# Opening of a linear attention with y and z in single pieces, attention steps of the first batch moved by one, and the last sum joined to its norm

## The chip, the cores and the metric

The kernel runs on one core of one Trainium2 chip. The metric is the device time of one execution in microseconds (us). The times shown are the median of three runs and one more execution under the hardware profiler. Five engines work side by side: TensorE (PE, with its weight loads listed as PEld), VectorE (DVE), ScalarE (ACT), GpSimd (POOL) and SyncE (SP, which issues DMAs). Each runs its own instructions in the order in which the program issues them, and waits on semaphores for the others.

## The reference

Eight batches of 512 tokens with 128 channels pass a linear attention and then a dense mixture of eight experts, each behind norms:

```python
x = x + layernorm(attn(layernorm(x)))      # attn has a norm, softmax and residual of its own
x = x + layernorm(ffn(layernorm(x)))

# attn: 4 heads of 32
xn = (x - mean) / sqrt(var + EPS) * gamma + beta
q, k, v = split(xn @ w_qkv)
q = q * 32 ** -0.5
k = softmax(k, over the tokens)
out = ((k.T @ v) applied to q) @ w_out + b_out
return out + x

# ffn: every token goes through all 8 experts, 128 -> 512 -> 128
for wg, wu, wd in experts:
    acc = acc + (silu(x @ wg) * (x @ wu)) @ wd
```

All data are float32. Inputs and weights are random; gamma, beta and b_out are not trivial.

## The kernel before, in words

**Stages.** A batch is worked on as 4 groups (NJ) of 128 tokens, tokens on the partitions in the attention, channels on the partitions in the experts. The experts are 32 steps (8 experts by 4 slices of 128 hidden units). A step multiplies the transposed tokens zT by a slice of wg (g, L902) and of wu (u, L903), 512 columns at once; ACT takes Silu of g into sg (L905); DVE multiplies by u into h (L926). The down projections are gathered over 16 steps and then run together in `down_pairs` (L797) from h and from sums `t` of pairs of h that POOL makes (L940 to L942); sums of the down weights, `ws`, are made once (`weight_sums`, L755). A bank of PSUM holds one g or u; the tags g and u have two banks each, the tag ps two, accA and accB one each. In the half steps every third step takes accA and accB in place of g and u.

**Units.** The list `units` first has batch 0 for steps 0 to 15, its first 256 tokens and then its second 256 (the half steps, 256 columns wide), then batch 0 whole for steps 16 to 31, then the batches 1 to 6 whole, and batch 7 whole up to step 24 and in halves after that.

**Opening.** `opening()` runs the attention of batch 0 directly, in an order written by hand, for both halves, as far as the first half's zT. Its parts: the norms of x (`pair_stats`), keys and their maximum (kmax, L370), exp (L373), values, context (c_ps), the matrix m (L418) that joins context and output weights, and then, for each half, the generator `after_m`, whose stages are separated by `yield`: the residual in y's bank by an identity matmul (L631), y by qT and m (L634), y's statistics (`norm_stats`, L177 to L183), the covariance of x and y, from which the next norm's scale rstd2 is had without statistics of x2 (L648 to L658), the normed yn and the sum x2 (L661), z (`norm_apply`, L252), z's transposes (L261) and the copies into zT (L671 and L673). `next(first)` and `next(second)` run one stage of a half. `keep_warm` issues matmuls whose results are not read, and `prepare` derives small weights for the later batches. The statistics of batch 1 (`bn`, `moments`, `powers`) are also computed in the opening.

**Plan.** `plan` gives, for every unit, a list of calls for each step. They are issued after the step's g, u, sg and h, and before the down projections that fall due. In the first unit they run the second half's stages, then batch 1's attention: norm, turn (32x32 transposes on DVE and a bounce through DRAM by SP), bias, affine, keys (key product, kmax, exp and the turn of the exponentials), with weight sums of the experts 0 to 4 on POOL in between. In the second unit four stages of `context` follow, and in the third `values` and the norms after it. Exp and Silu are in different activation tables, so that ACT loads a table before and after the keys' exp.

**End.** The last half of batch 7 is gathered in an `End` with one bank for each of its two groups. `finish` takes the statistics of both, norms them on DVE, adds x2 on POOL (group 0) and DVE (group 1), and stores them through the queues of SP and ACT.

Of the kernel before, what the change touches and what calls it, by code (L numbers as in the profile page):

```python
# [9 lines left out]
F32 = mybir.dt.float32  # L10
# [6 lines left out]
def kernel(  # L17
# [40 lines left out]
    nc = tc.nc  # L58
# [80 lines left out]
    def prepare():  # L139


        t = ps_acc.tile([P, N], F32, tag="accB", name="w_ps")
        nc.tensor.transpose(t[:, :C], w_qkv_sb[:, 0:C], ident)
        nc.scalar.mul(wqT, t[:, :C], QSCALE)
        nc.scalar.mul(gwv, w_qkv_sb[:, 2 * C : 3 * C], gamma_sb)
        yield
        nc.tensor.matmul(t[:, :1], w_qkv_sb[:, 2 * C : 3 * C], beta_sb, start=True, stop=True)
        bv = const.tile([P, 1], F32, name="bv")
        nc.scalar.copy(bv, t[:, :1])
        bvw = work.tile([P, C], F32, tag="gs", name="bvw")  # L150
        nc.scalar.mul(bvw, w_out_sb, bv)
        yield
        nc.tensor.matmul(t[:, :C], heads, bvw, start=True, stop=True)
        nc.scalar.copy(mb, t[:, :C])
        yield
# [57 lines left out]
    def scales(stats, name, pair=False):  # L213
        return powers(*moments(stats, name, pair), name)

    def moments(stats, name, pair=False):
        n = 2 * NJ if pair else NJ
        mv = small.tile([P, NJ, 2], F32, tag=f"mv{NJ}", name=f"mv_{name}")
        for j in range(NJ):
            nc.vector.bn_aggr(mv[:, j, :], stats[:, j, :])  # L220
        ve = small.tile([P, n], F32, tag=f"sve{n}", name=f"ve_{name}")
        nc.vector.tensor_scalar_add(ve[:, :NJ], mv[:, :, 1], EPS)
        if pair:
            nc.vector.scalar_tensor_tensor(
                ve[:, NJ:], ve[:, :NJ], EPS, mv[:, :, 1], ALU.mult, ALU.add
            )
        nm = small.tile([P, n], F32, tag=f"snm{n}", name=f"nm_{name}")
        for i in range(0, n, NJ):
            nc.vector.tensor_scalar(nm[:, i : i + NJ], mv[:, :, 0], -1.0, None, ALU.mult)  # L229
        return ve, nm  # L230

    def powers(ve, nm, name):


        n = ve.shape[1]
        rstd = small.tile([P, n], F32, tag=f"srstd{n}", name=f"rstd_{name}")
        nc.gpsimd.tensor_tensor(rstd, ve, mhalf[:, :n], ALU.pow)  # L237
        nc.gpsimd.tensor_tensor(nm, nm, rstd, ALU.mult)
        return rstd, nm
# [58 lines left out]
    def flat(t):  # L298
        return t.rearrange("p j c -> p (j c)")
# [3 lines left out]
    def opening():  # L303
# [19 lines left out]
        z = work.tile([P, NJ, C], F32, tag="z", name="z_0")  # L323
        zT = zp.tile([P, NQ, NJ, Q], F32, tag="zT", name="zT_0")
        kmax = small.tile([P, 3], F32, tag="kmax0", name="kmax_0")
# [12 lines left out]

        keep_warm(warm, 5)
        keep_warm(w_qkv_sb[:, : N // 2])  # L340
        nc.scalar.copy(junk, warm[:, :1])
# [21 lines left out]

        first_norm(0)
        for h in H:
            k_ps.append(bank(f"k_ps{h}", "ps" if h else "u"))
            nc.tensor.matmul(
                k_ps[h][:, :W], w_qkv_sb[:, C : 2 * C], xnT[:, COL[h]], start=True, stop=True
            )
            nc.vector.tensor_reduce(kmax[:, h : h + 1], k_ps[h][:, :W], AX.X, ALU.max, negate=True)  # L370
        nc.vector.tensor_tensor(kmax[:, 2:3], kmax[:, 0:1], kmax[:, 1:2], ALU.min)
        for h in H:
# [4 lines left out]
        for h in H:  # L377
# [7 lines left out]
            nc.vector.tensor_copy(v[:, COL[h]], v_ps[h][:, :W])  # L385
        next(first)
        for h in H:
            t = bank(f"ek_ps{h}", "u" if h else "g")
# [14 lines left out]
        nc.scalar.mul(qT[:, COL[0]], q_ps[0][:, :W], QSCALE)  # L403

        after = attentions[1] = Attention(1)
        after.s = bn(after.x[:, :3], "1_1")
        ctxT = work.tile([P, C], F32, tag="ctxT", name="ctxT_0")
# [8 lines left out]
        nc.vector.reciprocal(rsum, ksum[:, 2:3])  # L416
        bn(after.x[:, 3:], "1_1", after.s, 3)
        nc.vector.tensor_scalar(m, m_ps[:, :C], rsum, None, ALU.mult)  # L418
        next(first)
        next(second)  # L420
        next(second)
        moment = moments(after.s, "1_1", pair=True)
        weights = prepare()
# [7 lines left out]
        next(first)  # L431
        after.sc = powers(*moment, "1_1")
        keep_warm(flat(yn[:, J[0]]), 2)
        next(first)
        for _ in first:
# [34 lines left out]
    class Attention:  # L470
# [26 lines left out]

        def keys(self):
            b = self.b
            k_ps = ps.tile([P, N], F32, tag="ps", name=f"k_ps_{b}")  # L500
            nc.tensor.matmul(k_ps, w_qkv_sb[:, C : 2 * C], self.xnT, start=True, stop=True)  # L501
            kmax = small.tile([P, 1], F32, tag="kmax", name=f"kmax_{b}")
            nc.vector.tensor_reduce(kmax, k_ps, AX.X, ALU.max, negate=True)
            ekT = work.tile([P, N], F32, tag="ekT", name=f"ekT_{b}")
            ksum = small.tile([P, 1], F32, tag="ksum", name=f"ksum_{b}")
# [54 lines left out]
    class Last:  # L560
# [6 lines left out]
        def blocks(self):  # L567
# [3 lines left out]
                t.rearrange("p a (s j k) -> p a s j k", s=2, j=2),  # L571
                self.sums[len(self.f)].rearrange("c (s a j i) -> c a s j i", s=2, a=NQ, j=2),
            )
# [47 lines left out]
    def after_m(h, lo, hi, xt, s1, qT, m, x1b, x2, yn, z, zT):  # L621
# [4 lines left out]
        n = hi - lo  # L626
        pool, tag = (ps_gu, "u") if lo else (ps, "ps")
        y_ps = pool.tile([P, N], F32, tag=tag, name=f"y_ps_0_{lo}")
        for j in range(lo, hi):
            cols = slice((j - lo) * C, (j - lo + 1) * C)  # L630
            nc.tensor.matmul(y_ps[:, cols], ident, x1b[:, j, :], start=(j == lo), stop=False)  # L631
        yield
        for j in range(lo, hi):
            nc.tensor.matmul(  # L634
                y_ps[:, (j - lo) * C : (j - lo + 1) * C], qT[:, j * P : (j + 1) * P], m,
                start=False, stop=(j == hi - 1),
            )
        y = y_ps[:, : n * C].rearrange("p (j c) -> p j c", c=C)
        yield
# [5 lines left out]
        mv, rstd, ve = norm_stats(y, f"3_0_{lo}", keep=True)  # L645
        yield
        for j in range(n):
            nc.vector.scalar_tensor_tensor(  # L648
                z[:, lo + j], xt[:, lo + j], mvx[:, j, 0:1], y[:, j], ALU.subtract, ALU.mult,
                accum_out=cov[:, j : j + 1],  # L650
            )
        nc.vector.tensor_scalar(cov, cov, 2.0 / C, None, ALU.mult)
        nc.vector.reciprocal(rv, ve)
        nc.vector.tensor_tensor(rv, rv, mv[:, :, 1], ALU.mult)
        nc.vector.tensor_tensor(rv, rv, vex[:, :n], ALU.add)
        nc.gpsimd.tensor_tensor(t, rstd, cov, ALU.mult)
# [7 lines left out]
        yield  # L664
        norm_apply(z[:, r], x2[:, r], (mvx, rstd2))
        yield
        z_ps = transpose4(flat(z[:, r]), f"z_ps_0_{lo}")
        for j in range(1 if lo else n):
            cp = nc.vector.tensor_copy if j else nc.scalar.copy
            if lo:  # L670
                cp(zT[:, :, r], by_block(z_ps[:, : n * P], n))  # L671
            else:
                cp(zT[:, :, j], z_ps[:, j * P : (j + 1) * P].rearrange("c (a i) -> c a i", a=NQ))  # L673
        zTs[0] = zT

    class End:
# [42 lines left out]
        def finish(self):  # L719
# [4 lines left out]
            dst = out[b].rearrange("(p j) c -> p j c", j=NJ)  # L724
            s = [norm_stats([f], f"5_{b}_{self.lo + j}") for j, f in enumerate(self.f)]
            for j, f in enumerate(self.f):
                norm_apply([fn[:, j]], [f], s[j])
                (nc.vector if j else nc.gpsimd).tensor_tensor(
                    o[:, j, :], fn[:, j, :], x2s[b][:, self.lo + j], ALU.add
                )  # L730
                (nc.scalar if j else nc.sync).dma_start(dst[:, self.lo + j], o[:, j, :])
# [69 lines left out]
    def plan(b, lo, begin):  # L801
# [18 lines left out]
        if b == 0 and begin == 0:  # L820
            if not lo:
                second = rest.pop()
                go = lambda: next(second, None)
                at(0, go, a.norm)
                at(1, go)
                at(3, a.turn)
                at(4, go)
                at(6, go)
                at(8, go)
                for i, e in enumerate((0, 1, 2, 3, 4)):  # L830
                    at(2 + 2 * i, lambda e=e: weight_sums(nc.gpsimd, [e]))
                at(9, a.bias)
                at(13, a.affine)
                at(14, a.keys)
            else:
                for i in range(12, 16):
                    at(i, a.context)
# [28 lines left out]
        else:  # L866
            at(16, a.values)
            at(17, a.stats3, a.scales3, second.stats, second.scales, a.residual)
            at(17, lambda: weight_sums(nc.vector, [5, 6, 7]), second.norm, second.turn)
# [10 lines left out]
    for n, (b, lo, hi, begin, end) in enumerate(units):  # L880
        if lo == begin == 0 and b + 2 < B:
            xs[b + 2] = load_x(b + 2)
        zT = zTs[b][:, :, lo:hi]
        whole = hi - lo == NJ
        last = b == B - 1 and not whole
        cols = (hi - lo) * P
        if whole:
            zT = zT.rearrange("c a (h j) i -> c h a (j i)", h=2)
# [91 lines left out]
```

## Time and profile before

| what | us |
|---|---|
| median of 3 runs (lowest, highest) | 693.56 (693.36, 693.69) |
| the profiled execution | 693.51 |
| its span, first to last instruction | 691.60 |
| PE busy in the span | 682.9 |
| first expert matmul (L902) | 19.53 |
| last matmul ends, about | 686.6 |
| last DMA issue starts | 688.97 |

Start times in the profile count from the span's start. A line of the order of time gives start, length, engine, line and operation with output and inputs, the count of instructions that were merged, and in brackets how long the engine had been idle and who released it. Matmuls of float32 show as two instructions for one matmul of the program. Busy time of engines that nobody waits for does not set the time.

### The profile page before, as it was taken

The page shows a single profiled execution, that of the slowest core. Times are in us where ns is not written, and L with a number is a line of the kernel's source. Part 1 is how long each engine was busy: PE and PEld are TensorE (multiplying, and loading weights), DVE is VectorE, ACT ScalarE, POOL GpSimd, SP SyncE. Part 2 cuts the span into 40 slices and gives each one's busy share as a digit, 9 for nine tenths or more (in the row PEclk, how much of TensorE's full clock was granted, in tenths as well). Part 3 has the DMA queues.
Part 4 walks back from the last instruction along what each step waited for, and adds up shares of the span by engine and source line. Part 5 has one row for each costly group of instructions (what it writes and reads, how often), then busy time and mean ns, then how long its engine had stood idle before and what let it go on. Part 6 is the DMA issues. An engine that isn't in the chain of part 4 may idle for free.

```text
span 691.6 us, 9214 instructions
## 1 busy us (share of the span) xinstructions
PE 682.9 (99%) x3175; PEld 374.3 (54%) x3175; DVE 298.3 (43%) x810; ACT 247.9 (36%) x475; POOL 424.6 (61%) x524
## 2 busy tenths in 40 slices
PE   9999999999999999999999999999999999999997
PEld 6786455454554545545455544545445454544576
DVE  6656433543236432563325624256332534134135
ACT  4552441433424333344332434244351423122221
POOL 4779773767548574495726766377673857546521
PEclk9999999999999999999999999999999999999999
DMA  8610201020010200102001010111001010010010
GB/s 265 196 31 1 76 20 58 16 93 0 31 61 1 92 0 31 61 16 78 0 31 61 30 65 0 51 41 57 22 16 63 14 47 1 1 61 1 15 55 24
DMA packets 36672, 30.82 MB, mean 45 GB/s; under 512 B 3985, under 2 KB 28049, under 8 KB 36625
## 3 DMA queue, kind: packets, MB, share of 16 engines
q1 hardware_dynamic: 36336, 30.03, 13.5%
q8 instruction: 25, 0.41, 0.2%
q10 hardware_dynamic: 288, 0.20, 0.1%
q14 instruction: 23, 0.18, 0.1%
HBM read 18.42 MB, written 11.80 MB: 44 GB/s over the span
## 4 chain that ended last, share of the span: by engine, by line
PE 96%; DVE 1%; ACT 1%; DMA 0%; issue 0%; POOL 0%; DVEq 0%; ACTq 0%
PE g L902 32%; PE u L903 31%; PE accA L797 16%; PE accB L797 12%; PE y_ps L528 1%; PE g_ps L443 1%; PE k_ps L501 1%; PE end L699 1%; DMA x<-in_L_attn_x_dram 0%; PE end_A L699 0%; ACT xh L245 0%; PE wa_ps L464 0%; PE end_B L699 0%; PE m_ps L458 0%; PE c_ps L452 0%
## 5 line engine op out<-in xcount | busy, mean ns | idle before, releaser
L926 DVE TENSOR_TENSOR h<-sg,u 128x512 f32<-128x512 f32 (+1 forms) x264 | 172.6, 655 | 352.0 <-PE u L903 340.4
L905 ACT ACTIVATE sg<-g 128x512 f32<-128x512 f32 (+1 forms) x280 | 156.3, 560 | 377.7 <-PE g L902 353.8
L902 PE MATMUL g<-zT,wg 128*128 128x512 f32 (+1 forms) x560 | 267.5, 559 | 1.4 <-ACT sg L905 0.7
L903 PE MATMUL u<-zT,wu 128*128 128x512 f32 (+1 forms) x560 | 265.7, 556 | 0.9 <-DVE h L926 0.9
L940 POOL TENSOR_TENSOR t<-h 128x512 f32<-128x512 f32 x124 | 157.2, 1268 | 158.4 <-DVE h L926 158.4
L903 PEld LDWEIGHTS u<-zT,wu 128*128 128x128 f32 x560 | 106.1, 190 | 115.2 <-issue 109.5
L902 PEld LDWEIGHTS g<-zT,wg 128*128 128x128 f32 x560 | 101.2, 190 | 98.9 <-issue 95.6
L797 PE MATMUL accB<-t,ws 128*64 128x256 f32 x496 | 138.2, 381 | 0.0
L797 PE MATMUL accA<-h,wd 128*64 128x256 f32 x496 | 128.1, 381 | 0.0
L941 POOL TENSOR_TENSOR t<-h,t 128x256 f32<-128x256 f32 x124 | 90.1, 726 | 9.7
L942 POOL TENSOR_TENSOR t<-h,t 128x256 f32<-128x256 f32 x124 | 90.0, 726 | 9.7
L797 PEld LDWEIGHTS accA<-h,wd 128*64 128x64 f32 x496 | 66.6, 137 | 45.2 <-issue 6.4
L797 PE MATMUL accB<-h,ws 128*64 128x256 f32 x248 | 73.8, 379 | 0.0
L797 PE MATMUL accA<-t,ws 128*64 128x256 f32 x248 | 73.8, 379 | 0.0
L797 PEld LDWEIGHTS accB<-t,ws 128*64 128x64 f32 x496 | 66.6, 137 | 0.0
L237 POOL TENSOR_TENSOR rstd<-ve,mhalf 128x4 f32<-128x4 f32 (+1 forms) x28 | 32.8, 1173 | 18.4 <-DVE nm L229 16.3
L797 PEld LDWEIGHTS accB<-h,ws 128*64 128x64 f32 x248 | 34.0, 137 | 17.9
L797 PE MATMUL accB<-t,wd 128*64 128x256 f32 x124 | 36.9, 379 | 0.0
L797 PE MATMUL accA<-t,wd 128*64 128x256 f32 x124 | 36.9, 379 | 0.0
L797 PEld LDWEIGHTS accA<-t,ws 128*64 128x64 f32 x248 | 34.0, 137 | 0.0
L797 PEld LDWEIGHTS accB<-t,wd 128*64 128x64 f32 x124 | 17.0, 137 | 9.0
L516 POOL TENSOR_TENSOR x<-x,bias_sb 128x128 f32<-128x128 f32 x28 | 11.9, 455 | 15.3 <-ACT x L245 15.3
(177 smaller groups left out, 414.3 us busy)
## 6 DMA issues: line engine op xcount, KB each, us to landing
wg<-in_L_ffn_Wg_dram SPq DMA_DIRECT2D x8, 256.0 KB, 6.0
wu<-in_L_ffn_Wu_dram SPq DMA_DIRECT2D x8, 256.0 KB, 5.9
wd<-in_L_ffn_Wd_dram SPq DMA_DIRECT2D x8, 256.0 KB, 6.1
bounce<-f_blkA SPq DMA_DIRECT2D x8, 256.0 KB, 2.0
fA<-bounce SPq DMA_DIRECT2D x32, 64.0 KB, 2.0
bounce<-f_blkB SPq DMA_DIRECT2D x8, 256.0 KB, 2.1
fB<-bounce SPq DMA_DIRECT2D x32, 64.0 KB, 2.0
x<-in_L_attn_x_dram SPq DMA_DIRECT2D x7, 256.0 KB, 2.8
```

What stands on the lines that cost most here:

```text
L237: nc.gpsimd.tensor_tensor(rstd, ve, mhalf[:, :n], ALU.pow)
L443: nc.tensor.matmul(g_ps[:, :C], xh[:, j, :], ek[:, :, j * Q : (j + 1) * Q], start=(j == 0), stop=(j == NJ - 1),)
L501: nc.tensor.matmul(k_ps, w_qkv_sb[:, C : 2 * C], self.xnT, start=True, stop=True)
L516: nc.gpsimd.tensor_tensor(self.x1[:, j], self.x1[:, j], bias_sb, ALU.add)
L797: nc.tensor.matmul(o, w, r, start=start, stop=stop)
L902: nc.tensor.matmul(g_ps[:, :cols], wg_sb[e][:, w], zT, start=True, stop=True)
L903: nc.tensor.matmul(u_ps[:, :cols], wu_sb[e][:, w], zT, start=True, stop=True)
L905: nc.scalar.activation(sg[:, :cols], g_ps[:, :cols], AF.Silu)
L926: nc.vector.tensor_tensor(flat(h), sg[:, :cols], u_ps[:, :cols], ALU.mult)
L940: nc.gpsimd.tensor_tensor(t2[:, 0:2], h2[:, 1::2], h2[:, 0:2], ALU.subtract)
L941: nc.gpsimd.tensor_tensor(t2[:, 2], h2[:, 3], t2[:, 0], ALU.subtract)
L942: nc.gpsimd.tensor_tensor(t2[:, 3], h2[:, 2], t2[:, 2], ALU.subtract)
```

## The change

In the opening, the first half's y is kept in two banks, one for each group of 128 tokens (ps and accB), and its z is normed, transposed and copied one group after the other, through a bank each; zT of batch 0 is laid out group by group, and the way in which the sums of batch 0 are read back at its end follows that. w_ps of `prepare` goes from accB to a g bank. The small operations on rv in `after_m` come ahead of the products for cov. The statistics of batch 1 are taken in four single steps between other work, and `moments` and `powers` become `scales` again, called ahead of m. One warm-up matmul on w_qkv becomes one on a constant.

In the plan, the second half's stages come at the steps 0, 2, 5, 7, 10 in place of 0, 1, 4, 6, 8, and batch 1's turn at 4 in place of 3. The key product with its maximum stays at step 14, and exp with what follows goes to step 15. The contexts come at 13, 14, 15 and 16 in place of 12 to 15, and the values at 17 in place of 16.

In `finish`, ACT computes mean minus f while POOL computes the scale, and one DVE instruction multiplies by the scale and subtracts the product from x2.

```diff
     def prepare():
-        t = ps_acc.tile([P, N], F32, tag="accB", name="w_ps")
+        t = ps_gu.tile([P, N], F32, tag="g", name="w_ps")
...
     def scales(stats, name, pair=False):
-        return powers(*moments(stats, name, pair), name)
...
-        return ve, nm
-
-    def powers(ve, nm, name):
...
     def opening():
...
-        zT = zp.tile([P, NQ, NJ, Q], F32, tag="zT", name="zT_0")
+        zT = zp.tile([P, NJ, NQ, Q], F32, tag="zT", name="zT_0")
...
-        keep_warm(warm, 5)
-        keep_warm(w_qkv_sb[:, : N // 2])
+        keep_warm(warm, 6)
...
         first_norm(0)
+        after = attentions[1] = Attention(1)
+        after.s = bn(after.x[:, :1], "1_1")
         for h in H:
...
             nc.vector.tensor_reduce(kmax[:, h : h + 1], k_ps[h][:, :W], AX.X, ALU.max, negate=True)
+            if h == 0:
+                bn(after.x[:, 1:2], "1_1", after.s, 1)
...
         next(first)
+        bn(after.x[:, 2:3], "1_1", after.s, 2)
         for h in H:
             t = bank(f"ek_ps{h}", "u" if h else "g")
...
         nc.scalar.mul(qT[:, COL[0]], q_ps[0][:, :W], QSCALE)
-
-        after = attentions[1] = Attention(1)
-        after.s = bn(after.x[:, :3], "1_1")
+        bn(after.x[:, 3:], "1_1", after.s, 3)
...
         nc.vector.reciprocal(rsum, ksum[:, 2:3])
-        bn(after.x[:, 3:], "1_1", after.s, 3)
+        after.sc = scales(after.s, "1_1", pair=True)
         nc.vector.tensor_scalar(m, m_ps[:, :C], rsum, None, ALU.mult)
         next(first)
         next(second)
         next(second)
-        moment = moments(after.s, "1_1", pair=True)
         weights = prepare()
...
         next(first)
-        after.sc = powers(*moment, "1_1")
         keep_warm(flat(yn[:, J[0]]), 2)
-        next(first)
         for _ in first:
             pass
...
     def after_m(h, lo, hi, xt, s1, qT, m, x1b, x2, yn, z, zT):
...
+        if lo:
+            y_ps = ps_gu.tile([P, N], F32, tag="u", name=f"y_ps_0_{lo}")
+            y = pieces(y_ps[:, : n * C].rearrange("p (j c) -> p j c", c=C))
+        else:
+            banks = [(ps, "ps"), (ps_acc, "accB")]
+            y = [p.tile([P, N], F32, tag=t, name=f"y_ps_{t}")[:, :C] for p, t in banks]
+        for j in range(n):
+            nc.tensor.matmul(
+                y[j], ident, x1b[:, lo + j, :], start=(lo == 0 or j == 0), stop=False
+            )
+        yield
+        for j in range(n):
+            nc.tensor.matmul(
+                y[j], qT[:, (lo + j) * P : (lo + j + 1) * P], m,
+                start=False, stop=(lo == 0 or j == n - 1),
+            )
         yield
...
-        for j in range(n):
-            nc.vector.scalar_tensor_tensor(
-                z[:, lo + j], xt[:, lo + j], mvx[:, j, 0:1], y[:, j], ALU.subtract, ALU.mult,
-                accum_out=cov[:, j : j + 1],
-            )
-        nc.vector.tensor_scalar(cov, cov, 2.0 / C, None, ALU.mult)
         nc.vector.reciprocal(rv, ve)
         nc.vector.tensor_tensor(rv, rv, mv[:, :, 1], ALU.mult)
         nc.vector.tensor_tensor(rv, rv, vex[:, :n], ALU.add)
+        for j in range(n):
+            nc.vector.scalar_tensor_tensor(
+                z[:, lo + j], xt[:, lo + j], mvx[:, j, 0:1], y[j], ALU.subtract, ALU.mult,
+                accum_out=cov[:, j : j + 1],
+            )
+        nc.vector.tensor_scalar(cov, cov, 2.0 / C, None, ALU.mult)
...
+        else:
+            for j in range(n):
+                norm_apply([z[:, j]], [x2[:, j]], (mvx[:, j : j + 1], rstd2[:, j : j + 1]))
+                t = (ps_gu if j else ps).tile([P, N], F32, tag="g" if j else "ps", name=f"z_ps_0{j}")
+                nc.tensor.transpose(t[:, :P], z[:, j], ident)
+                (nc.vector.tensor_copy if j else nc.scalar.copy)(
+                    zT[:, j], t[:, :P].rearrange("c (a i) -> c a i", a=NQ)
+                )
...
     def finish(self):
...
-            s = [norm_stats([f], f"5_{b}_{self.lo + j}") for j, f in enumerate(self.f)]
+            s = []
             for j, f in enumerate(self.f):
-                norm_apply([fn[:, j]], [f], s[j])
-                (nc.vector if j else nc.gpsimd).tensor_tensor(
-                    o[:, j, :], fn[:, j, :], x2s[b][:, self.lo + j], ALU.add
+                s.append(norm_stats([f], f"5_{b}_{self.lo + j}"))
+                nc.scalar.activation(
+                    fn[:, j], f, AF.Identity, bias=s[j][0][:, 0, 0:1], scale=-1.0
+                )
+            for j in range(self.n):
+                nc.vector.scalar_tensor_tensor(
+                    o[:, j, :], fn[:, j], s[j][1], x2s[b][:, self.lo + j], ALU.mult, ALU.subtract,
+                    reverse1=True,
                 )
                 (nc.scalar if j else nc.sync).dma_start(dst[:, self.lo + j], o[:, j, :])
...
                 at(0, go, a.norm)
-                at(1, go)
-                at(3, a.turn)
-                at(4, go)
-                at(6, go)
-                at(8, go)
+                at(2, go)
+                at(4, a.turn)
+                at(5, go)
+                at(7, go)
+                at(10, go)
...
-                at(14, a.keys)
+                at(14, a.product)
+                at(15, a.softmax)
             else:
-                for i in range(12, 16):
+                for i in range(13, 16):
                     at(i, a.context)
...
-            at(16, a.values)
-            at(17, a.stats3, a.scales3, second.stats, second.scales, a.residual)
+            at(16, a.context)
+            at(17, a.values, a.stats3, a.scales3, second.stats, second.scales, a.residual)
```

Not shown are the split of `keys` into `product` and `softmax`, the unchanged path of `after_m` for the second half, and the indexing of zT and of the sums of batch 0.

More of the change, by code (lines that the diff above doesn't have):

```diff
@@ L213, in scales @@
     def scales(stats, name, pair=False):
-        return powers(*moments(stats, name, pair), name)
-    def moments(stats, name, pair=False):
         n = 2 * NJ if pair else NJ
@@ L229, in moments @@
             nc.vector.tensor_scalar(nm[:, i : i + NJ], mv[:, :, 0], -1.0, None, ALU.mult)
-        return ve, nm
-    def powers(ve, nm, name):
-        n = ve.shape[1]
         rstd = small.tile([P, n], F32, tag=f"srstd{n}", name=f"rstd_{name}")
@@ L498, in keys, with product @@
         def keys(self):
+            self.product()
+            self.softmax()
+        def product(self):
             b = self.b
@@ L503, in keys, with softmax @@
             nc.vector.tensor_reduce(kmax, k_ps, AX.X, ALU.max, negate=True)
+            self.k = k_ps, kmax
+        def softmax(self):
+            b = self.b
+            k_ps, kmax = self.k
             ekT = work.tile([P, N], F32, tag="ekT", name=f"ekT_{b}")
@@ L571, in blocks @@
                 t.rearrange("p a (s j k) -> p a s j k", s=2, j=2),
-                self.sums[len(self.f)].rearrange("c (s a j i) -> c a s j i", s=2, a=NQ, j=2),
+                self.sums[len(self.f)].rearrange(
+                    "c (s a j i) -> c a s j i" if self.b else "c (s j a i) -> c a s j i",
+                    s=2, a=NQ, j=2,
+                ),
             )
@@ L626, in after_m @@
         n = hi - lo
[L627 to L631, printed above, removed]
+        if lo:
[8 more added lines that the diff above has]
+            )
         yield
-        for j in range(lo, hi):
+        for j in range(n):
             nc.tensor.matmul(
-                y_ps[:, (j - lo) * C : (j - lo + 1) * C], qT[:, j * P : (j + 1) * P], m,
-                start=False, stop=(j == hi - 1),
+                y[j], qT[:, (lo + j) * P : (lo + j + 1) * P], m,
+                start=False, stop=(lo == 0 or j == n - 1),
             )
-        y = y_ps[:, : n * C].rearrange("p (j c) -> p j c", c=C)
         yield
@@ L646, in after_m @@
         yield
+        nc.vector.reciprocal(rv, ve)
+        nc.vector.tensor_tensor(rv, rv, mv[:, :, 1], ALU.mult)
+        nc.vector.tensor_tensor(rv, rv, vex[:, :n], ALU.add)
         for j in range(n):
             nc.vector.scalar_tensor_tensor(
-                z[:, lo + j], xt[:, lo + j], mvx[:, j, 0:1], y[:, j], ALU.subtract, ALU.mult,
+                z[:, lo + j], xt[:, lo + j], mvx[:, j, 0:1], y[j], ALU.subtract, ALU.mult,
                 accum_out=cov[:, j : j + 1],
@@ L652, in after_m @@
         nc.vector.tensor_scalar(cov, cov, 2.0 / C, None, ALU.mult)
-        nc.vector.reciprocal(rv, ve)
-        nc.vector.tensor_tensor(rv, rv, mv[:, :, 1], ALU.mult)
-        nc.vector.tensor_tensor(rv, rv, vex[:, :n], ALU.add)
         nc.gpsimd.tensor_tensor(t, rstd, cov, ALU.mult)
@@ L664, in after_m @@
         yield
[L665 to L673, printed above, removed]
+        if lo:
+            norm_apply(z[:, r], x2[:, r], (mvx, rstd2))
+            yield
+            z_ps = transpose4(flat(z[:, r]), f"z_ps_0_{lo}")
+            nc.scalar.copy(
+                zT[:, r], z_ps[:, : n * P].rearrange("c (j a i) -> c j a i", j=n, a=NQ)
+            )
[7 more added lines that the diff above has]
+                )
         zTs[0] = zT
@@ L882 @@
             xs[b + 2] = load_x(b + 2)
-        zT = zTs[b][:, :, lo:hi]
+        zT = zTs[b][:, :, lo:hi] if b else zTs[0][:, lo:hi]
         whole = hi - lo == NJ
@@ L886 @@
         cols = (hi - lo) * P
-        if whole:
+        if whole and b:
             zT = zT.rearrange("c a (h j) i -> c h a (j i)", h=2)
```

## The prediction

> **What bounds the kernel now.** I read the page first, then busy time by stretch, then PE's waits, then the order of time on each engine around every wait. The page's first table and clock row:
>
> ```profile
> PE 682.9 (99%) x3175; PEld 374.3 (54%) x3175; DVE 298.3 (43%) x810; ACT 247.9 (36%) x475; POOL 424.6 (61%) x524
> ...
> PEclk9999999999999999999999999999999999999999
> ```
>
> TensorE is busy 682.9 of 691.6 us at full clock. By stretches, from 57 to 686 us it is busy 629.00 of 629.00: nothing there can be shortened by the change, which alters no matmul of the experts. What can move is the opening (first L902 matmul at 19.53), the few waits up to 57 us, and the tail after the last matmul (686 to 691.6). PE's waits, us in total, times, longest:
>
> ```profile
> PE u L903 <- DVE h L926: 0.9, 2, 0.7
> ...
> PE g L902 <- ACT sg L905: 0.7, 1, 0.7
> PE g L902 <- DVE zT L673: 0.7, 1, 0.7
> ```
>
> After the first L902 these are all: two u waits (0.15 at 21.24, 0.72 at 24.82) and a g wait (38.67); the last line is the end of the opening. The chain of waits through the opening's last step (start, length, what):
>
> ```profile
> 17.65 0.34 DVE z L252
> ...
> 18.12 0.36 DVE z L252
> ...
> 18.52 0.34 PE z_ps L261
> ...
> 18.89 0.28 ACT zT L673
> ...
> 19.18 0.30 DVE zT L673
> ...
> 19.53 0.48 PE g L902
> ```
>
> The reader should see a row of single steps: both transposes, then one copy, then the other.
>
> **What the Trainium skill says.** "PSUM — Partial Sum Buffer", section "PSUM bank collisions raise a hardware error": two engines may not be in one bank at once, and dependencies are set to keep them apart. The trace agrees: DVE's copy waits 0.72 for ACT's, out of the same bank. "SBUF — State Buffer", section "Who interferes with whom": VectorE and GpSimd share a port pair, exclusively, and tensor_scalar is among the operations that can take it. The trace fits: L252's second z starts 0.47 after the first, with GpSimd's 1.64 pow (17.52) beside it. "ScalarE: Activation LUTs", section "What ACT_TABLE_LOAD costs": 1.283 us and a drain of 1.38 for every switch. The trace has the 1.28 but no drain: Silu's load at 36.94 is followed by its activation at 38.23. "TensorE: Matmul & The Clock Gate", section "Why this matters for your kernels": idle gaps over about 3 us cost the clock. No gap here or below is that long, so I price no slower matmuls.
>
> **Opening, statistics of batch 1.** One bn_stats (0.27) goes ahead of kmax 0, one ahead of kmax 1, one ahead of the ek copy: VectorE waited 0.35, 0.32 and 0.43 at these places, so they fit. The first needs batch 1's x: issued at 3.53, landing 4.5 later, 8.03. It then runs 8.05 to 8.3, kmax 0 slips from 8.07 to 8.25, and kmax 1 (8.82, when its matmul is done) holds. Cost 0, with no margin.
>
> The means and scales move ahead of m (L418). VectorE's order of time:
>
> ```profile
> 12.64 0.16 DVE L416 RECIPROCAL rsum<-ksum 128x1 f32<-128x1 f32 x1
> 12.72 0.27 DVE L210 BATCH_NORM_STATS2 stats<-x 128x6 f32<-128x128 f32 x1
> 13.12 0.35 DVE L418 TENSOR_SCALAR m<-m_ps,rsum 128x128 f32<-128x128 f32 x1
> 13.39 0.37 DVE L220 BATCH_NORM_AGGREGATE mv<-stats 128x2 f32<-128x6 f32 x4
> ```
>
> Before, four aggregates and four small operations (13.39 to 14.31) lay under y's matmuls. Now they start at 12.72 and their starts span 0.77, so with 0.08 for the last issue m starts at 13.56 and ends at 13.91; y's first matmul comes at 13.96, not 13.62: +0.34. GpSimd's pow (1.64) and product (0.20) come at 13.57 and end at 15.48, just before y's own pow needs GpSimd: 0.
>
> **Opening, y in two banks.** Both pieces were read at 14.34, after 0.68 of matmuls. Now y0 is done after 0.49 (L410's pair, alone) at 14.45, y1 at 14.67, and their statistics overlap the matmuls. ve starts at 15.24 instead of 15.08: 0.18 won of the 0.34. Keeping w_ps in a g bank, and a sixth constant warm-up in place of one on w_qkv (same width), cost nothing: the transposes that follow at 6.30 are PE work behind the same number of passes.
>
> **Opening, order of the covariance.** Before, GpSimd's first product ran at 16.13 while VectorE still did reciprocal, product and sum. Now these three come first and cov last: counted with the trace's steps (0.2 for a dependent small operation, 0.27 for a product), VectorE ends 0.13 later, and GpSimd does product, sum (0.28 each to the next) and pow (0.69) only after that. Relative to ve, z starts 0.42 later: +0.42; the lower bound is 0.1, if GpSimd takes the pair faster.
>
> **Opening, z in pieces.** From z0's start to L902 was 1.88. Now z1 starts 0.26 after z0 (as two xh of L252 do, no pow beside them), ends at 0.61, is transposed in its own bank from 0.65 to 0.98, copied from 1.01 to 1.31 while ACT's copy of the other piece is done, and L902 starts at 1.36: -0.52. **Sum of the opening: 0.34 - 0.18 + 0.42 - 0.52 = +0.06**; bounds -0.35 and +0.5.
>
> **Half steps, second half of batch 0.** cov moves from step 1 to 2. The wait at 24.82 is for h of step 3, behind h1, cov and h2; the same work in another order ends at the same time: 0. The transpose (0.70) goes from step 3 to 4 and yn (0.72) from 4 to 5. y's second half holds one of the two u banks until yn is read. VectorE: h4 25.63, transpose 25.97, h5 26.61, yn 26.94 to 27.66. u of step 7, at 27.52 now, wants that bank: 27.70, **+0.18** (0, or 1.05 if u of step 6 draws it). SP's bounce moves from 25.41 to about 26.7; its loads land by some 33, when affine (33.40) wants them: 0.
>
> GpSimd is the queue to watch:
>
> ```profile
> 26.54 0.45 POOL L755 TENSOR_TENSOR ws<-wd,ws 128x128 f32<-128x128 f32 x1
> 26.95 0.72 POOL L661 TENSOR_TENSOR x<-yn,x 128x256 f32<-128x256 f32 x1
> ```
>
> x2 (L661) stood behind one expert's weight sums; now it stands behind two, 1.78 each. pow ends at 25.78, the sums at 29.31, x2 at 30.03, and z runs to about 31.06 (0.99 for two, as at 27.70). Its transposes, moved from step 8 to 10, come up at 30.70; the second would start at 30.81 and starts at 31.10: **+0.29** (0 to 0.6). h of steps 8 to 10 wait behind z, but u of step 11, at 31.64, finds h8 done at 31.4.
>
> **Exp.** The keys' product stays at step 14, the softmax goes to 15. ACT's order of time there:
>
> ```profile
> 34.49 1.28 ACT L506 ACT_TABLE_LOAD   x1
> 36.14 0.69 ACT L506 ACTIVATE ekT<-k_ps,kmax 128x512 f32<-128x512 f32 x1 [0.37 <-DVE kmax L503]
> ...
> 36.94 1.28 ACT L905 ACT_TABLE_LOAD   x1
> ```
>
> and PE's answer to it:
>
> ```profile
> 38.67 0.70 PE L902 MATMUL g<-zT,wg 128*128 128x256 f32 x2 [0.70 <-ACT sg L905]
> ```
>
> ACT was away from 34.47 to 38.22, and PE ran three steps ahead (two g banks and the spare) plus k's 0.97: g of step 18 was late by 38.67 - 37.80 = 0.87. Now sg15 runs first (to 36.22), then load 1.28, exp and read 0.80, load 1.28: sg16 ends at 39.99 and g of step 19 starts at 40.05. PE, with k's matmul already spent, is ready at 38.67: 1.38 late, **+0.51**. The 0.37 wait for kmax is saved, but the cover of k's 0.97 is lost. Bounds: -0.3, if steps run further ahead than the banks say, and +0.8.
>
> Contexts and values one step later are the same matmuls. Pair sums on GpSimd then start about 1.3 later than 39.81; the eighth ends at 62.64 now and PE's last round of that group begins near 66: covered. The other axis order of batch 0's sums is one transpose in covered time: 0.
>
> **The end.** Before: pow of B ends at 688.18, fn (0.41), o (0.29), DMA issue at 688.97:
>
> ```profile
> 688.20 0.41 DVE L252 TENSOR_SCALAR fn_last<-end_B,mv,rstd 128x128 f32<-128x128 f32 x1 [0.20 <-POOL rstd L183]
> 688.65 0.29 DVE L728 TENSOR_TENSOR o_last<-fn_last,x 128x128 f32<-128x128 f32 x1
> ```
>
> Now ACT, idle since 685.1, subtracts the mean (about 0.4, under the pow), and one scalar_tensor_tensor follows at 688.20 (0.29 to 0.34): issue at 688.53, **-0.44** (-0.5 to -0.35). ACT pays no table load: L245's Identity at 20.55 follows Silu without one.
>
> **Sum.** 0.06 + 0.18 + 0.29 + 0.51 - 0.44 = +0.60. The profiled execution took 693.51 (span 691.60 and 1.91 around it; 0.05 under the median 693.56): 694.1. A measurement can tell about 0.2% here, 1.39 us: below 692.17 is faster, above 694.95 slower.
>
> **Rivals.** (1) The moved steps are hidden and the opening gains its lower bound: 693.51 - 0.35 - 0.44 = 692.7. For: banks or order may give PE more lead than I count. Against: the 0.70 at 38.67 shows how little lead there is. 0.30. (2) Slower: batch 1's x lands late. Its bn_stats now stands ahead of kmax on VectorE, and everything of the opening comes behind it there. From 8.05 each microsecond costs one. The weights around it take 5.2 to 6.1 from issue; at 5.9 it lands at 9.43: +1.40, 695.5. Against: it took 4.5 in this run. 0.10. (3) The y bank is drawn by u of step 6: 1.05 for 0.18, and the transposes' 0.29 vanishes: 694.7. 0.07. (4) Faster: as (1), and cov's move frees the 0.72 wait at 24.82: 692.0. Against: equal work ahead of h3. 0.04. My forecast holds 0.49.
>
> **Numbers.** Faster is (4), 0.04; slower is (2) and a tail of the forecast, 0.12; the rest, 0.84, is within 0.2%. The range takes in (1), (3) and the terms' bounds, and leaves out (2) and (4): 692.6 to 694.9.
>
> **What would show it.** m starting near 13.56; L902 near 19.6; GpSimd's L661 near 29.3; a g wait near 40 of 1.2 idle instead of 0.70; 0.4 less from the last pow to the last issue. I am wrong if z starts before 18.0, if the wait on sg shrinks, or if the first bn_stats of batch 1 waits beyond 8.3.

## The result, and the profile after

The changed kernel takes 694.84 us (median of 16 runs, 694.67 to 695.2), the kernel before 693.50 beside it. The ratio is 1.0019, with a 95% interval of 1.0012 to 1.0027: slower by 1.34 us, clear of zero, and just inside the 0.2% that the prediction had called no change. The profiled execution took 694.86, its span 692.9 us.

The page of the changed kernel has the same PE busy time and the same clock as before:

```profile
PE 682.9 (99%) x3175; PEld 374.4 (54%) x3175; DVE 298.6 (43%) x809; ACT 248.8 (36%) x477; POOL 425.7 (61%) x523
...
PEclk9999999999999999999999999999999999999999
```

So all of the difference is in waits and at the two ends. PE's waits in the changed kernel (us in total, times, longest):

```profile
PE g L925 <- ACT sg L928: 1.2, 1, 1.2
PE u L926 <- DVE h L949: 0.8, 1, 0.8
...
PE y_ps_ps L645 <- ACT qT L410: 0.5, 1, 0.5
PE g L925 <- ACT zT L687: 0.4, 1, 0.4
```

The wait of g on sg grew from 0.7 to 1.2, and y's matmuls wait where they did not; only the wait at the end of the opening is shorter. (The view puts y's wait down to ACT's qT, which is done at 13.90. But y starts 0.15 after m's end in both kernels, at 13.62 after 13.47 before and at 13.99 after 13.84 now, so m fits as what it waits for.)

The opening is best counted from the first bn_stats, which starts when batch 0's x lands: 3.48 in the profile before, 3.19 in the one after, and from 3.17 to 3.62 over all profiles of this study, for reasons that the profiles don't show. From there:

| us from the first bn_stats to | before | after |
|---|---|---|
| kmax of the second half | 5.34 | 5.61 |
| m | 9.64 | 10.31 |
| ve of y (L181) | 11.60 | 12.07 |
| z of the first group | 14.17 | 15.29 |
| first expert matmul | 16.05 | 16.71 |

VectorE at the first row. Batch 1's statistics now stand ahead of kmax, and the first of them waits for x:

```profile
8.07 0.29 DVE L210 BATCH_NORM_STATS2 stats<-x 128x6 f32<-128x128 f32 x1 [0.63 <-DMA x<-in_L_attn_x_dram]
8.28 0.41 DVE L366 TENSOR_REDUCE kmax<-k_ps 128x1 f32<-128x256 f32 x1
8.60 0.28 DVE L210 BATCH_NORM_STATS2 stats<-x 128x6 f32<-128x128 f32 x1
8.80 0.41 DVE L366 TENSOR_REDUCE kmax<-k_ps 128x1 f32<-128x256 f32 x1
```

The scales of batch 1 ahead of m, again VectorE in order of time:

```profile
13.36 0.23 DVE L228 TENSOR_SCALAR nm<-mv 128x4 f32<-128x4 f32 x2
13.50 0.34 DVE L415 TENSOR_SCALAR m<-m_ps,rsum 128x128 f32<-128x128 f32 x1
```

The chain of waits through the last part of the opening (start, length, what) now runs through POOL:

```profile
16.94 0.21 POOL cov L666
...
17.22 0.21 POOL cov L667
...
17.49 0.96 POOL cov L668
...
18.48 0.35 DVE z L245
...
18.88 0.34 PE z_ps L686
...
19.24 0.28 ACT zT L687
...
19.90 0.45 PE g L925
```

From z to the first expert matmul it takes 1.42 instead of 1.88: the pieces do what they say. But z starts late, and pow (L668) is 0.96 long, not 0.69 as before. In the half steps, POOL's x2 stands behind two experts' sums, as its order of time shows:

```profile
29.37 0.46 POOL L777 TENSOR_TENSOR ws<-wd,ws 128x128 f32<-128x128 f32 x1
29.79 0.73 POOL L671 TENSOR_TENSOR x<-yn,x 128x256 f32<-128x256 f32 x1
```

ACT around the first keys' exp, and PE's wait that follows:

```profile
36.85 0.38 ACT L928 ACTIVATE sg<-g 128x256 f32<-128x256 f32 x1 [1.37 <-PE g L925]
37.26 1.28 ACT L509 ACT_TABLE_LOAD   x1
38.55 0.69 ACT L509 ACTIVATE ekT<-k_ps,kmax 128x512 f32<-128x512 f32 x1
...
39.35 1.28 ACT L928 ACT_TABLE_LOAD   x1
```

```profile
41.08 0.70 PE L925 MATMUL g<-zT,wg 128*128 128x256 f32 x2 [1.24 <-ACT sg L928]
```

The 0.37 that exp had waited for kmax is gone, and PE waits longer all the same. At the end, one instruction stands between the last pow and the last issue:

```profile
689.73 0.35 DVE L749 SCALAR_TENSOR_TENSOR o_last<-fn_last,rstd,x 128x128 f32<-128x128 f32 x1 [0.26 <-POOL rstd L183]
690.12 0.36 ACTq L753 DMA_DIRECT2D out_dram<-o_last  x1
```

From the last round of end_A matmuls to that issue it is 3.21 us, before 3.58.

My theory after reading the two traces: the change costs in four places that do not depend on each other (scales ahead of m; the order of cov, which delays POOL in the opening and again in the half steps; the moved stages of the second half; exp one step later), and gains in two (the pieces, the end). The rival was that one lateness early in the kernel shows up again further on, so that undoing a later part alone would bring nothing.

### The profile page after: what moved, and what is told of

It is laid out like the page before. It is cut to its first block, busy times and chain, and to the rows that moved or that the text cites. A ratio compares the mean times of both kernels' runs of the same rounds, so it can differ in the third digit from the quotient of the medians.

```text
span 692.9 us, 9212 instructions
## 1 busy us (share of the span) xinstructions
PE 682.9 (99%) x3175; PEld 374.4 (54%) x3175; DVE 298.6 (43%) x809; ACT 248.8 (36%) x477; POOL 425.7 (61%) x523
## 4 chain that ended last, share of the span: by engine, by line
PE 95%; DVE 1%; POOL 1%; ACT 1%; DMA 1%; issue 1%; SPq 0%; POOLq 0%; DVEq 0%
PE g L925 32%; PE u L926 31%; PE accA L819 16%; PE accB L819 12%; PE y_ps L531 1%; PE g_ps L437 1%; PE k_ps L499 1%; DMA x<-in_L_attn_x_dram 1%; PE end L715 1%; POOL ws L777 0%; PE end_A L715 0%; POOL cov L668 0%; ACT xh L238 0%; PE end_B L715 0%; PE wa_ps L458 0%
```

## The experiments

Times are medians of 9 to 21 executions; the kernel before, beside them, took 693.52, 693.46 or 693.48. Single executions of one kernel scatter by 0.3 to 0.8 us: the changed kernel's lie between 694.67 and 695.20. With exp back, with the old order of cov and with the old stages, every execution was below that; the smaller differences rest on overlapping executions.

**The end alone**, in the kernel before (`finish` as in the change, nothing else):

```diff
-                norm_apply([fn[:, j]], [f], s[j])
-                (nc.vector if j else nc.gpsimd).tensor_tensor(
-                    o[:, j, :], fn[:, j, :], x2s[b][:, self.lo + j], ALU.add
...
+                nc.scalar.activation(
+                    fn[:, j], f, AF.Identity, bias=s[j][0][:, 0, 0:1], scale=-1.0
+                )
+            for j in range(self.n):
+                nc.vector.scalar_tensor_tensor(
+                    o[:, j, :], fn[:, j], s[j][1], x2s[b][:, self.lo + j], ALU.mult, ALU.subtract,
+                    reverse1=True,
```

> The kernel before with the changed end alone. Theory (the last issue comes earlier by the removed step): the last DMA issue starts 0.37 us sooner after the last round of end matmuls, as it did in the changed kernel (3.21 against 3.58), and the time falls by 0.37, to 693.1. Rival (part of it is lost behind the issue, since the changed kernel's span went on 2.78 us after its last issue instead of 2.63): the time falls by 0.2 only, to 693.3.

Measured: 693.26, down by 0.26 (ratio 0.9997, 0.9989 to 1.0005, so not clear of zero by itself). The issue is earlier as expected, 688.75 - 685.55 = 3.20 us after end_A. The median lies between the theory's 693.1 and the rival's 693.3. What follows the last issue is 2.46 to 2.83 us in the eleven profiles with the new end and 2.60 in the two with the old one, so that the 0.2 between theory and rival can't be settled.

**Exp at step 15 alone**, in the kernel before:

```diff
-                at(14, a.keys)
+                at(14, a.product)
+                at(15, a.softmax)
```

> The kernel before with the first keys' exp at step 15 and the key product left at step 14, nothing else. Theory (PE's lead no longer contains the key product while ACT is away): the wait of g on sg grows from 0.70 to about 1.25 us of idle, and the time rises by 0.5, to 694.0. Rival (the wait only grew in the changed kernel because its opening and half steps had pushed ACT and PE apart): 693.5, the wait stays near 0.7.

Measured: 694.04, up by 0.52. PE's waits in this kernel:

```profile
PE g L912 <- ACT sg L915: 1.2, 1, 1.2
```

**Exp back at step 14**, in the changed kernel:

```diff
-                at(15, a.softmax)
+                at(14, a.softmax)
```

> The changed kernel with exp back at step 14, nothing else. Theory: the wait of g on sg goes back to about 0.7 us of idle and the time falls by 0.55, to 694.3. Rival (as for the exp alone): no change, 694.8.

Measured: 694.33, down by 0.51, with the wait back at 0.7. The two runs agree with opposite signs, one with and one without the rest of the change: the term stands alone.

**One expert's sums ahead of x2 instead of two**, in the changed kernel:

```diff
-                for i, e in enumerate((0, 1, 2, 3, 4)):
-                    at(2 + 2 * i, lambda e=e: weight_sums(nc.gpsimd, [e]))
+                for i, e in zip((2, 6, 7, 8, 10), range(5)):
+                    at(i, lambda e=e: weight_sums(nc.gpsimd, [e]))
```

> The changed kernel with the weight sums of experts 1 to 4 issued at the steps 6, 7, 8 and 10 instead of 4, 6, 8 and 10, so that x2 stands behind one expert's sums on POOL and not two. Theory (z's transposes are late because x2 is queued behind the sums): x2 starts near 28.1 instead of 29.79, z is done before step 10, and the time falls by 0.4, to 694.4. Rival (the transposes themselves cost that at their new step, whatever z does): 694.8.

Measured: 694.60, down by 0.24. POOL reaches x2 sooner although the opening of this profile ended 0.30 later:

```profile
28.45 0.72 POOL L671 TENSOR_TENSOR x<-yn,x 128x256 f32<-128x256 f32 x1
```

The direction is that of the theory, the size is smaller, and single executions overlap (694.38 to 694.97). From u of step 10 to g of step 11 it was 0.96 in the changed kernel and is 0.65 now, as it was before at the old step; I had counted the transposes' own 0.22 as a loss. What they wait for is 0.31.

**The old order of cov**, in the changed kernel:

```diff
-        nc.vector.reciprocal(rv, ve)
-        nc.vector.tensor_tensor(rv, rv, mv[:, :, 1], ALU.mult)
-        nc.vector.tensor_tensor(rv, rv, vex[:, :n], ALU.add)
         for j in range(n):
...
         nc.vector.tensor_scalar(cov, cov, 2.0 / C, None, ALU.mult)
+        nc.vector.reciprocal(rv, ve)
+        nc.vector.tensor_tensor(rv, rv, mv[:, :, 1], ALU.mult)
+        nc.vector.tensor_tensor(rv, rv, vex[:, :n], ALU.add)
```

> The changed kernel with the order of the covariance put back (cov's products first, the operations on rv after them), nothing else. Theory (POOL's three operations wait for the last of VectorE's, and pow then meets x2's addition and takes 0.95 instead of 0.70): in the opening z comes some 0.5 us sooner after y's ve, and in the half steps POOL reaches x2 about 0.4 sooner, so that most of the lateness of z's transposes goes: together -0.8, to 694.0. Rival (order without effect, z waits for x2 anyway): 694.8.

Measured: 693.78, down by 1.06: the dearest single part. (The profile shows 0.87 of it: 0.59 in the opening and 0.28 from the first expert matmul to the last round of end_A.) From ve to z it is 2.62 instead of 3.22 (before 2.57). POOL's pow in this kernel:

```profile
17.41 0.70 POOL L668 TENSOR_TENSOR cov<-cov,mhalf 128x2 f32<-128x2 f32 x1
```

and VectorE's addition, which now comes after it:

```profile
17.67 0.43 DVE L671 TENSOR_TENSOR x<-yn,x 128x256 f32<-128x256 f32 x1
```

In the half steps x2 is sooner too (29.24), and z's transposes no longer wait (30.97, 0.40 long, where they took 0.69).

**The first statistics of batch 1 behind kmax 0**, in the changed kernel:

```diff
-        after.s = bn(after.x[:, :1], "1_1")
...
             if h == 0:
-                bn(after.x[:, 1:2], "1_1", after.s, 1)
+                after.s = bn(after.x[:, :1], "1_1")
```

and the two later calls take the groups 1, and 2 with 3.

> The changed kernel with the first bn_stats of batch 1 behind kmax 0 and the others one place later, nothing else. Theory (it waited 0.63 us for batch 1's x ahead of kmax 0, and kmax 1 came 0.27 later after the first statistics than in the kernel before): the distance from the first bn_stats to m falls from 10.31 to about 10.06 and the time by 0.25, to 694.6. Rival (kmax 1 is late for another reason, PE's): no change, 694.8.

Measured: 694.74, down by 0.10, with executions from 694.45 to 694.97, so that neither no change nor the 0.25 is ruled out. In its profile the distance to m is 10.06, as expected, so kmax 1 was late for the theory's reason there. How much it is late varies with the landing of batch 1's x. Counted from the first bn_stats, the statistics ahead of kmax could start at 4.88 to 4.91 in four profiles, the changed kernel's among them, at about 4.75 in two, and at 4.46 in the run on m below; kmax 1 is late by 0.27 to 0.30, by 0.13 to 0.17, and not at all. That may be why the time shows less than 0.25; it is not shown.

**The scales behind m**, in the changed kernel (`aggr` is the four bn_aggr, `moments` the small operations, `powers` POOL's part):

```diff
         bn(after.x[:, 3:], "1_1", after.s, 3)
+        after_mv = aggr(after.s, "1_1")
         ctxT = work.tile([P, C], F32, tag="ctxT", name="ctxT_0")
...
-        after.sc = scales(after.s, "1_1", pair=True)
         nc.vector.tensor_scalar(m, m_ps[:, :C], rsum, None, ALU.mult)
+        moment = moments(after_mv, "1_1", pair=True)
+        after.sc = powers(*moment, "1_1", part=slice(NJ, 2 * NJ))
+        after.sc_rest = lambda: powers(*moment, "1_1", part=slice(0, NJ), rstd=after.sc[0])
...
-                at(0, go, a.norm)
+                at(0, go, a.norm, a.sc_rest)
```

> The changed kernel with batch 1's bn_aggr ahead of ctxT, the rest of its scales behind m, half of the powers at once and half after the first step; nothing else. Theory (the scales ahead of m hold m back by 0.42): the distance from m_ps to m closes, the distance from the first bn_stats to the first expert matmul falls from 16.71 to about 16.3, and the time by 0.4, to 694.4. Rival (the late m is covered by what comes later, pow and x2): 694.8.

Measured: 694.37, down by 0.47. m waits for its matmul again (the four bn_aggr stay ahead of it):

```profile
13.05 0.35 DVE L425 TENSOR_SCALAR m<-m_ps,rsum 128x128 f32<-128x128 f32 x1 [0.32 <-PE m_ps L418]
```

Its distance to the first expert matmul, 15.99, is better than expected by 0.3, because x landed early in this profile.

**The second half's stages back at 0, 1, 4, 6, 8 and turn at 3**, in the changed kernel:

```diff
-                at(2, go)
-                at(4, a.turn)
-                at(5, go)
-                at(7, go)
-                at(10, go)
+                at(1, go)
+                at(3, a.turn)
+                at(4, go)
+                at(6, go)
+                at(8, go)
```

> The changed kernel with the second half's stages back at the steps 0, 1, 4, 6, 8 and turn at 3; exp stays at step 15. Theory (the half steps cost 0.64 in the changed kernel by the moved stages: 0.08 at u of step 4, 0.25 at u of step 7 whose bank y holds a step longer, 0.31 at z's transposes): the waits at step 7 and at the transposes go, and the time falls by 0.6, to 694.2. Rival (the later end of the opening's own work, POOL's and VectorE's, causes them, and they come back in some form): 694.6 or more.

Measured: 694.39, down by 0.45. The wait at u of step 7 and the longer one at step 4 are gone. Of the 0.31 at the transposes, 0.18 stays (0.83 from u of step 8 to g of step 9, before 0.65): the late pow of the new order of cov still delays x2. So the rival was right on a part of it. In the run with the old order of cov it is 0.67 from u of step 10 to g of step 11, so almost no wait is left.

**Contexts back at 12 to 15 and values at 16**, in the changed kernel:

```diff
-                for i in range(13, 16):
+                for i in range(12, 16):
...
-            at(16, a.context)
-            at(17, a.values, a.stats3, a.scales3, second.stats, second.scales, a.residual)
+            at(16, a.values)
+            at(17, a.stats3, a.scales3, second.stats, second.scales, a.residual)
```

> The changed kernel with the contexts back at the steps 12 to 15 and the values at 16, nothing else. Theory (the same matmuls one step later, with no wait in either kernel): no change, 694.8. Rival (a part of what the change costs lies here, in what follows the values at step 17): at least 0.2 less, 694.6.

Measured: 694.90, no change. This part of the change is free.

**What gains, without what costs.** The changed kernel with the edits for the scales, for the first statistics, for cov's order, for the stages and for exp, all together, each as its diff above (with the statistics in the groups 0, 1, and 2 with 3); pieces and end stay.

> The pieces of y and z and the end of the changed kernel, with what cost time taken back: the first bn_stats behind kmax 0, bn_aggr of batch 1 ahead of ctxT and the rest of its scales behind m, half of their powers at once and half after the first step, cov's products first, the half steps at 0, 1, 4, 6, 8 with turn at 3, and exp at step 14. Theory: the distance from the first bn_stats to the first expert matmul falls to 15.4 (before 16.05, after 16.71), the half steps and exp cost what they cost before, the end gains 0.25: 692.6, faster than before by 0.9. Rival (the opening's pieces gain nothing once another engine is the next to be late): 693.2, the end alone.

Measured: 692.30, ratio to before 0.9984 (0.9977 to 0.9990), 1.16 faster. Undone one at a time, the five parts gave 0.10 + 0.47 + 1.06 + 0.45 + 0.51 = 2.59 us; together they give 694.84 - 692.30 = 2.54. From the first bn_stats to the first expert matmul it is 15.59, 0.46 less than before but not the 15.4 expected, because the two z are 0.46 apart again (below). With the end's 0.38 and 0.05 less in between, the profile accounts for 0.89 of the 1.16. Then the stages moved further:

```diff
-                at(1, go)
-                at(3, a.turn)
-                at(4, go)
-                at(6, go)
-                at(8, go)
-                for i, e in enumerate((0, 1, 2, 3, 4)):
-                    at(2 + 2 * i, lambda e=e: weight_sums(nc.gpsimd, [e]))
+                at(3, go)
+                at(4, go)
+                at(5, a.turn)
+                at(7, go)
+                at(9, go)
+                for i, e in zip((5, 6, 8, 10, 12), range(5)):
+                    at(i, lambda e=e: weight_sums(nc.gpsimd, [e]))
```

> As the run before, with the second half's stages at 0, 3, 4, 7, 9, turn at 5 and the weight sums at 5, 6, 8, 10, 12. Theory (the wait of u in step 4 for h of step 3 comes from cov's seven operations ahead of that h on VectorE; one step later than the change put it, they stand behind it): the 0.7 us wait near 25 us goes, and x2 is ahead of all weight sums: 692.0. Rival (another u wait takes its place, since one u bank is held by y): 692.6, as the run before.

Measured: 691.81, ratio 0.9975 (0.9966 to 0.9985): 1.65 faster than before and 3.0 faster than the changed kernel. PE's waits in it:

```profile
PE g L937 <- ACT sg L940: 0.7, 1, 0.7
...
PE u L938 <- DVE h L961: 0.3, 2, 0.2
```

The 0.7 at u of step 4 has become 0.15.

## Why the prediction was right, and what it mis-sized

The kind was right: no gain, a loss within what I had called no change, 694.84 in a range of 692.6 to 694.9. But it lies 0.06 under the upper edge, and that it does is partly luck: the sum of +0.60 was short by 0.74, nearly every term that missed did so to the same side, and the opening as a whole came to +0.66 where its bounds were -0.35 and +0.5. The kinds of cost and gain were right; the sizes of several terms were not. Term by term, with what the runs and the profile give:

| term of the prediction | predicted | found |
|---|---|---|
| statistics of batch 1 ahead of kmax | 0 | +0.10 (time, not clear of zero), +0.27 in the profile |
| scales ahead of m | +0.34 | +0.47 (time), +0.40 in the profile |
| y in two banks | -0.18 | -0.20 |
| order of cov, opening | +0.42 | +0.60 to 0.65 |
| z in pieces | -0.52 | -0.46 |
| half steps | +0.47 | +0.64 (0.08, 0.25, 0.31) |
| exp at step 15 | +0.51 | +0.51 (time), +0.54 in the profile |
| end | -0.44 | -0.26 (time), -0.37 to the issue |

The profile's own terms add up to 1.41 with the span's ends in them: +0.66 in the opening, +0.64, +0.54 for exp, -0.37 to the last issue, and the start 0.29 earlier and the tail 0.23 longer, which vary from run to run. Of that, 0.03 comes back before the last round; the spans differ by 1.38. With the times where they exist, the found column gives 0.10 + 0.47 - 0.20 + 0.60 - 0.46 + 0.64 + 0.51 - 0.26 = 1.40, against 1.34 measured; it mixes times and profiles, so the agreement is rough. The terms are nearly additive, except that cov's order and the half steps share x2's wait.

**Order of cov** failed by the most. The step counted POOL's pow at 0.69. VectorE's last operation came later, POOL's pow slid from 0.26 ahead of x2's addition to 0.03 behind its start, and took 0.95. The 0.42 forecast and this 0.25 make 0.67, where 0.65 was found. I had the addition and the pow in one paragraph and did not lay one over the other. The same order also delays POOL in the half steps; that I had (pow's end at 25.78; it came at 26.27), but not as a cost of cov's order. It is 1.06 together, the largest single part, where I had looked for 0.42.

**Scales ahead of m** and **statistics ahead of kmax.** The first was right in mechanism and size: with kmax on time, in the run on the first statistics, m comes 10.06 after the start, or 13.54 at the start of 3.48 for which 13.56 was forecast. The second was priced at nothing "with no margin"; the landing of x has no fixed place, and the margin was used up in most profiles. The slower rival of the prediction was this mechanism; its size was far smaller than the 1.40 named. (The price of that rival rested on weights that take 5.2 to 6.1 from issue; the two loads issued right after x took 4.64 and 4.91 in the profile before.)

**Half steps.** u of step 7 waited for y's bank, 0.15, and a wait costs PE another 0.10 before its pace is back (0.53 from that u to the next g instead of 0.43), which I had not counted. The transposes waited 0.31 for 0.29 predicted. Step 4's u came 0.08 later than the "0" of the prediction.

**Exp** was right in mechanism and size: PE ran three steps ahead and no further, and k's matmul was no longer under ACT's absence.

**The end** gained what its issue shows, less 0.07 of the forecast because the joint instruction took 0.35 where I had used the lower end of 0.29 to 0.34. That the median gives only 0.26 stays open within the scatter of the tail.

**A reading that fell**, though no number hung on it but z's step: I took the 0.47 between the two z before for contention with POOL's pow. In the run without the costs, POOL is idle from 17.44 to 21.68, and its z shows

```profile
17.53 0.80 DVE L255 TENSOR_SCALAR z<-x,mv,cov 128x128 f32<-128x128 f32 x2
```

with the second one at 17.99, 0.46 after the first. In the changed kernel the distance is 0.26 with POOL equally idle. What makes it is open; it is not POOL. So the 0.26 forecast for the pieces came true in the changed kernel, but not for its reason, and in the run without the costs z to the first expert matmul is 1.61, not 1.42.

## What to carry to other kernels

When small operations change places, lay each engine's new order over the other engines' and see which operation is last at each join: here the order of six operations on VectorE was worth 1.06 us, and four parts that cost hid two that gained. Undo the parts one at a time before judging such a bundle; a version that keeps the two useful parts, undoes the others and puts the stages behind the h that PE waits for is 3.0 us faster than the whole. An engine's absence (two table loads and exp) costs its length less PE's lead, so extra matmuls belong inside that window: with the key product inside it PE waited 0.70, without it 1.24.

## What the runs showed of the hardware that I had not expected

- POOL's pow on 128x2 took 0.95 to 0.96 in all seven kernels in which it started 0.02 to 0.03 after VectorE's addition of two SBUF tensors (128x256), and 0.69 to 0.70 in the six in which it started 0.25 to 0.26 ahead of it. The addition took 0.42 to 0.43 either way. Behind VectorE's product h, which reads u from PSUM and had started 0.16 earlier (pow at 24.51 in the profile before), pow took 0.69. The Trainium skill's page "SBUF — State Buffer", section "Who interferes with whom", says that a VectorE instruction with two SBUF inputs contends with a GpSimd instruction that reads SBUF, and that the order of issue decides who waits. These runs agree for the case in which VectorE comes first by a hair, though pow grew by 0.25 and not by the 0.4 that was left of the addition; where POOL came first, VectorE's addition showed no wait.
- VectorE's z on 128x128 took 0.34 to 0.35 in the opening, alone or beside POOL's pow. In the half steps of the changed kernel, beside POOL's sums of 128x128 tiles, the two took 0.46 and 0.61 (at 30.55 and 30.93). That the sums are the cause was not tested.
- One load's landing has no fixed place: over the 13 profiles of this study, each of another kernel, batch 1's x landed 4.3 to 4.9 us after its issue.
